# Image keys and values of two cross-attention layers: one level of seven products, or two nested levels with streamed weight operands

## The chip, the cores and the metric

The kernel runs on one core of a Trainium2 chip. The metric is the time of one execution on the device in microseconds (us). The kernel before was run three times, and the profile is one further execution of it, recorded by the hardware profiler. The engines are called PE (matrix products; PEld is its weight load), DVE (vector engine), ACT (scalar engine), POOL (GpSimd) and SP (which only issues DMAs here). L637 is line 637 of the kernel.

## The reference

Two cross-attention layers follow each other on `x` (8 batches, 100 queries, 640 channels). Both attend to the same context of 722 tokens of 1024 channels: 77 text tokens and 645 image tokens. There are 20 heads of 32 channels. Everything is fp32. Per layer, cut to what matters:

```
q = heads(x @ Wq)
k, v       = heads(text @ Wk), heads(text @ Wv)
k_ip, v_ip = heads(ip @ Wk_ip), heads(ip @ Wv_ip)     # 645 x 1024 times 1024 x 640, per batch
out = softmax(q k^T / sqrt(32)) v + softmax(q k_ip^T / sqrt(32) [+ sem / 2]) v_ip [* mask]
x   = out @ Wo + bias + x
```

The bracketed parts are in the second layer alone: `sem` is a score of the image tokens that comes from the text (softmax of q against the text keys over all channels, times the text, times the image tokens), and `mask` scales each query's image part. The image keys and values `k_ip`, `v_ip` don't depend on `x`. They are 2 layers x 8 batches x 2 products, the largest part of the arithmetic.

## The kernel before

**Seven products.** A product of two matrices, each cut into 2 x 2 quarters, can be had from seven products of quarters instead of eight, if sums of quarters are formed first and the results are summed afterwards. `seven` (L191 to L235) does this for one product. Its seven steps are named after the product they make, in the order 1, 6, 2, 7, 5, 4, 3, and they use five PSUM banks' names a, b, a, c, d, e, d: products 2 and 3 go on in the bank of 1 and 5. After each product the result leaves PSUM: by an ACT copy (L202, L211) or a DVE add with the partial result (L207, L217, L222, L228, L233). The sums of weight quarters (`weight_sums`, `w4_sums`, DVE) are made once per layer and stay in SBUF, the sums of token quarters (`block_sums`, `third_sum`, `fourth_sum`; L241, L242, L587, L599, DVE) once per block.

**Production.** The image tokens of a pair of batches (`PAIRS`) are the two halves of the rows. A pair has five blocks of tokens: four of 128 and a fifth of 133. `pair_tasks` lists its work. For v the tokens are the weight operand (128 x 128) and the weights move, 320 columns, or 397 where a text part lies beside them in layer 0 (L637). For k the weights are the weight operand and two blocks of tokens move, 256 columns, or 133 for the fifth block (L667). The fifth chunk of 128 output channels of k is made for both layers at once. Results go by POOL's DMA queue to DRAM (`v_d` at L652, `k_d` at L691 and L694). The last pair of layer 1 has its own order (`two_chunks`, `fifth_chunk`, L786 to L841). Pair 0 is made ahead of the attention; the others in it.

**Attention.** `ORDER` lists 80 iterations (u, c): u is one of 16 layer-and-batch units, c one of five chunks of four heads. An iteration loads k and v, makes the scores (L994), the softmax over text and image (DVE L1003 to L1057, ACT L1017 to L1049), the transposes (L1099, emptied by DVE L1106 or ACT L1104) and the product with v (L1122). The steps that have no product of PE in them are kept in a list `later`, and are emitted one at a time, so that they lie between products. The out projection (L904), the next layer's q (L923) and the `sem` steps are placed in fixed slots of iterations.

**Order.** The order of PE, DVE and ACT is the order of the program (`manual_schedule`). POOL's and SP's order is left to the scheduler. `production` gives each pair a stretch of ten iterations, shifted by `AHEAD` = 1.2; `spread` places its tasks there by estimated times, so that each iteration gets the same work. `next_task` emits one element of `later` before each product; `apart` lets one product come before a transposition or another small piece.

**PSUM.** Of the eight banks, two belong to products (`ps_pj`), two to transposes and other pieces of the attention (`ps_pt`), and four to scores. Before the attention the products have six (`ps_first`).

Of the kernel before, what the change touches and what calls it, by code (L numbers as in the profile page):

```python
# [36 lines left out]
BLOCKS = [(j * P, (j + 1) * P if j < NB - 1 else NI) for j in range(NB)]  # L37
NX = NI - (NB - 1) * P
# [8 lines left out]
def two_layer_xattn(  # L47
# [21 lines left out]
    wpool = ctx.enter_context(tc.tile_pool(name="w", bufs=1))  # L69
    cpool = ctx.enter_context(tc.tile_pool(name="ctx", bufs=2))  # L70
    spool = ctx.enter_context(tc.tile_pool(name="sums", bufs=1))
    opool = ctx.enter_context(tc.tile_pool(name="made", bufs=2))
    dram = ctx.enter_context(tc.tile_pool(name="scratch", bufs=1, space=bass.MemoryType.DRAM))

# [11 lines left out]

    ident = const.tile([P, P], F32, tag="ident", name="ident")
# [6 lines left out]
    W = {}  # L94

    def load_quarters(kind, src, n):

        rows = src.rearrange("(k p) n -> p k n", p=P)
        for i in range(2):
            for j in range(2):  # L100
                load_quarter(kind, rows, n, i, j)


    WITH_TEXT = ("wv00", "wv01", "wv10", "wvt4")
    wide = {}

    def weight_tile(tag, n, name=None):
        w = HC + NT if tag in WITH_TEXT else HC if tag[:2] == "wv" else n
        wide[tag] = wpool.tile([P, HK, w], F32, tag=tag, name=name or tag)
        return wide[tag][:, :, :n]  # L110

    def load_quarter(kind, rows, n, i, j):
        t = weight_tile(f"w{kind}{i}{j}", n)
        nc.sync.dma_start(t, rows[:, HK * i : HK * (i + 1), n * j : n * (j + 1)])
        W[kind, f"b{i + 1}{j + 1}"] = t

    def load_text(us):

        for i, (tag, h) in zip((0, 0, 1, 1), (("wv00", 0), ("wv10", 1), ("wv01", 0), ("wvt4", 1))):
            b = us[i] % B  # L120
            nc.sync.dma_start(
                wide[tag][:, :, HC:],
                text_t[HK * h : HK * (h + 1)].rearrange("k p n -> p k n")[:, :, b * NT : (b + 1) * NT],
            )

    def text_sum():
        t = wide["wvt4"][:, :, HC:]
        nc.gpsimd.tensor_tensor(t, t, wide["wv01"][:, :, HC:], ALU.subtract)

    def weight_sums(kind, n):  # L130

        b11, b12, b21, b22 = (W[kind, f"b{x}"] for x in ("11", "12", "21", "22"))
        t2, t3, t4 = (weight_tile(f"w{kind}t{x}", n) for x in (2, 3, 4))
        W[kind, "t1"], W[kind, "t2"], W[kind, "t3"], W[kind, "t4"] = b12, t2, t3, t4
        return [
            lambda: nc.vector.tensor_tensor(t3, b22, b12, ALU.subtract),
            lambda: nc.vector.tensor_tensor(t2, t3, b11, ALU.add),
            lambda: nc.vector.tensor_tensor(b12, b12, b11, ALU.subtract),
            lambda: nc.vector.tensor_tensor(t4, b21, t2, ALU.subtract),
        ]  # L140
# [4 lines left out]
    def load_wk(src):  # L145
        load_quarters("k", src, 2 * P)
        load_wk4(src)

    def load_wk4(src):
        W["k", 4] = wpool.tile([P, NCC, P], F32, tag="wk4", name="wk4")  # L150
# [3 lines left out]
    NPLACE = 3  # L154
    x_all = cpool.tile([P, NPLACE, 2, NCC, NX], F32, tag="x", name="x", bufs=1)
    placed = [0]

    s_all = spool.tile([P, 3, HK, 2, NX], F32, tag="s", name="s")

    def place_of(us, i):  # L160

        return (NB * PAIRS.index(us) + i) % NPLACE

    def quarters(at, n):
        return [x_all[:, at, i, HK * h : HK * (h + 1), :n] for i in range(2) for h in range(2)]

    def load_x(us, i):

        j = i % NB
        n0, n1 = BLOCKS[j]  # L170
        at = placed[0] % NPLACE
        placed[0] += 1
        for h, u in enumerate(us):
            nc.sync.dma_start(
                x_all[:, at, h, :, : n1 - n0], ip_t[u % B].rearrange("k p n -> p k n")[:, :, n0:n1]
            )
        assert at == place_of(us, i)
        return at

    ps_pj = ctx.enter_context(tc.tile_pool(name="ps_pj", bufs=2, space=PSUM))
    pj = []

    def product_ps(name):
        return pj[0].tile([P, 512], F32, tag="pj", name=name)

    def seven(name, product, area, beside=None):
# [6 lines left out]
        def flat(which):  # L195
            a = ps[which][:, :n]
            return a if len(c11.shape) == 2 else a.rearrange("p (r n) -> p r n", r=c11.shape[1])

        def first():
            ps["a"] = product_ps(f"{name}_a")  # L200
            product(ps["a"], 1, False)
            nc.scalar.copy(c11, flat("a"))  # L202

        def sixth():
            ps["b"] = product_ps(f"{name}_b")
            product(ps["b"], 6, False)
            nc.vector.tensor_tensor(c12, flat("b"), c11, ALU.add)  # L207

        def second():
            product(ps["a"], 2, True)  # L210
            nc.scalar.copy(c11, flat("a"))  # L211
            beside(2, ps["a"])

        def seventh():
            ps["c"] = product_ps(f"{name}_c")
            product(ps["c"], 7, False)
            nc.vector.tensor_tensor(c21, flat("c"), c12, ALU.add)  # L217

        def fifth():
            ps["d"] = product_ps(f"{name}_d")  # L220
            product(ps["d"], 5, False)
            nc.vector.tensor_tensor(c22, flat("d"), c21, ALU.add)  # L222
            beside(5, ps["d"])

        def fourth():
            ps["e"] = product_ps(f"{name}_e")
            product(ps["e"], 4, False)
            nc.vector.tensor_tensor(c21, flat("e"), c21, ALU.add)  # L228
            beside(4, ps["e"])

        def third():
            product(ps["d"], 3, True)
            nc.vector.tensor_tensor(c12, flat("d"), c12, ALU.add)  # L233

        return [first, sixth, second, seventh, fifth, fourth, third]  # L235

    TEXT_AT = {1: "wv00", 2: "wv10", 5: "wv01", 4: "wvt4"}
    WHICH = {1: "b11", 2: "b21", 3: "b22", 4: "t4", 5: "t1", 6: "t2", 7: "t3"}

    def token_sums(a11, a12, a21, a22, s1, s2, s3, s4):  # L240
        nc.vector.tensor_tensor(s1, a21, a22, ALU.add)  # L241
        nc.vector.tensor_tensor(s2, s1, a11, ALU.subtract)  # L242
        if s3 is not None:
            nc.vector.tensor_tensor(s3, a11, a21, ALU.subtract)
            nc.vector.tensor_tensor(s4, a12, s2, ALU.subtract)
        return {1: a11, 2: a12, 3: s4, 4: a22, 5: s1, 6: s2, 7: s3}

    def block_sums(us, j, pos):

        n = BLOCKS[j][1] - BLOCKS[j][0]  # L250
        a11, a12, a21, a22 = quarters(place_of(us, j), n)
        sums = [s_all[:, i, :, pos, :n] for i in range(3)]
        token_sums(a11, a12, a21, a22, sums[0], sums[1], None, sums[2])
# [4 lines left out]
    with ExitStack() as es:  # L258
        fp = es.enter_context(tc.tile_pool(name="first", bufs=1))
        pj.append(es.enter_context(tc.tile_pool(name="ps_first", bufs=6, space=PSUM)))  # L260
# [4 lines left out]
        for k in range(NC_):  # L265
            t = fp.tile([P, C], F32, tag="wr", name=f"wq0_{k}", bufs=NCC)
# [32 lines left out]
        for g in range(B // 2):  # L299
            t = fp.tile([P, 2, NC_, S], F32, tag="q", name=f"q0_{g}", bufs=2)  # L300
# [29 lines left out]
        def text_k(l):  # L330
            t = fp.tile([P, 2, 512], F32, tag="ev", name=f"kt4_{l}", bufs=2)
# [9 lines left out]
            for r in range(2):  # L341
                t = opool.tile([P, 2, 2, C // 2], F32, tag="made", name=f"kt_{l}_{r}")

                def product(ps, which, go_on, r=r):
                    for k in range(HK):
# [6 lines left out]
                for f in seven(  # L352
                    f"pskt_{l}_{r}", product, tuple(t[:, h, m, :TH] for h in range(2) for m in range(2))
# [7 lines left out]
        def text_v(l):  # L361

            t = fp.tile([P, 2, 512], F32, tag="ev", name=f"vtr_{l}", bufs=2)
# [17 lines left out]
        def text_v_blocks(l):  # L381
            for r in range(2):
                t = opool.tile([P, 2, 2, HC], F32, tag="made", name=f"vt_{l}_{r}")

                def product(ps, which, go_on, r=r):
                    for k in range(HK):
# [5 lines left out]
                for f in seven(f"psvt_{l}_{r}", product, tuple(t[:, h, m] for h in range(2) for m in range(2))):  # L392
# [6 lines left out]
        wl = {}  # L399

        def load_left(l):
            for k in range(NCC):
                wl[l, k] = fp.tile([P, C], F32, tag="wr", name=f"wl_{l}_{k}", bufs=NCC)
                nc.sync.dma_start(wl[l, k], wvi[l][k * P : (k + 1) * P, :])

        def left_v(l):

            ps = product_ps(f"psvl_{l}")
            for k in range(NCC):
                for m in range(2):  # L410
                    nc.tensor.matmul(
                        ps[64 * m : 64 * m + B * NL, :HC], lhsT=left_sb[:, k, :],
                        rhs=wl[l, k][:, m * HC : (m + 1) * HC],
# [27 lines left out]

        def all_of(parts):
# [3 lines left out]
        with tc.manual_schedule(engines=PINNED):  # L446
            text_sums()
            all_of(weight_sums("k", 2 * P))
            text_k(0)
            load_wk(wkt[1])  # L450
            v = weight_sums("v", HC)
            all_of(v[:2])
            text_v(0)
            all_of(v[2:])
            load_left(0)
            text_v_blocks(0)
            load_wv(wvt[1])
            all_of(weight_sums("k", 2 * P))
            text_k(1)
            load_quarters("k", wki[0], 2 * P)  # L460
            left_v(0)
            load_left(1)
            left_text()
            v = weight_sums("v", HC)
# [3 lines left out]
            for j in range(3):  # L468
# [960 lines left out]
```

## Time and profile before

| what | before |
|---|---|
| median of three runs | 2043.24 us (2042.67 to 2043.44) |
| span of the profiled execution | 2041.3 us |
| PE busy | 2024.2 us, 99%, clock 1.0 |
| DVE busy | 1129.4 us, 55% |
| ACT busy | 783.1 us, 38% |
| POOL busy | 274.2 us, 13% |
| DMA | 252.20 MB, mean 124 GB/s |
| PE, start to 205 us (q, text) | 202.98 busy |
| PE, 205 to 405 us (pair 0) | 198.41 |
| PE, 405 to 1341 us (iterations 0 to 39, layer 0) | 934.91 |
| PE, 1341 to 1909 us (iterations 40 to 69) | 565.64 |
| PE, 1909 us to the end | 122.21 |

The profiled execution's own time is its span, 2041.3 us; the median of the runs lies 1.9 us above it. A line of a timeline gives the start in us, the time for which the group was busy, the engine, the line of the kernel, the operation, the tiles (output <- inputs), the shape and how often; in brackets the idle time of the engine before it and what ended it. Several equal instructions in a row are merged into one line. Matmuls overlap: what one costs is the distance between starts, not its own duration. A line of the waits reads: engine, tile and line that waited, what ended the wait, total us, number, longest.

### The profile page before, as it was taken

The numbers are of one execution on the slowest core, as the hardware profiler recorded it, in microseconds if no ns is written. First come the engines' busy times: TensorE is split into PE (matmuls) and PEld (weight loads), VectorE is DVE, ScalarE is ACT, GpSimd is POOL, SyncE is SP. The second block draws the span as 40 slices with busy tenths as digits, with TensorE's granted clock in tenths as the row PEclk, the third lists the DMA queues.
The fourth block names the chain that finished last, engine by engine and source line by source line (L and its number), as shares of the span: only waits on it lengthen the run. The fifth ranks groups of instructions, "written<-read, shape, count | busy, mean of one in ns | idle before, by whom it ended". The sixth has DMA issues, their size and how long they took to land.

```text
span 2041.3 us, 38689 instructions
## 1 busy us (share of the span) xinstructions
PE 2024.2 (99%) x15162; PEld 1568.8 (77%) x15162; DVE 1129.4 (55%) x3048; ACT 783.1 (38%) x2245; POOL 274.2 (13%) x433
## 2 busy tenths in 40 slices
PE   9999999999999999999999999999999999999998
PEld 9676768776876867778678777777777778889877
DVE  2223322245555465554657665655665667778787
ACT  1001000033433343333434444444544455566676
POOL 0001212111111101111111001001010101111110
PEclk9999999999999999999999999999999999999999
DMA  9544323323432533325256354236342536545461
GB/s 341 154 131 147 108 75 93 99 66 93 117 99 71 157 102 108 89 83 156 90 131 172 92 164 121 82 100 183 99 118 81 148 95 174 147 138 152 124 189 55
DMA packets 296628, 252.20 MB, mean 124 GB/s; under 512 B 46654, under 2 KB 265586, under 8 KB 296446
## 3 DMA queue, kind: packets, MB, share of 16 engines
q1 hardware_dynamic: 274398, 181.19, 32.8%
q0 software_dynamic: 21776, 68.44, 9.3%
q8 instruction: 119, 1.95, 0.4%
q14 instruction: 63, 0.52, 0.1%
q10 hardware_dynamic: 272, 0.10, 0.0%
HBM read 180.74 MB, written 68.93 MB: 122 GB/s over the span
## 4 chain that ended last, share of the span: by engine, by line
PE 95%; DVE 4%; ACT 1%; issue 0%; DMA 0%; SPq 0%; DVEq 0%
PE psv_a L637 9%; PE psv_d L637 8%; PE pspt L1099 8%; PE psk_a L667 8%; PE psk_d L667 7%; PE sc L994 6%; PE psv_e L637 4%; PE pv L1122 4%; PE psk_b L667 4%; PE psk_c L667 4%; PE psv_b L637 4%; PE psv_c L637 4%; PE psk_e L667 4%; PE pso L904 3%; PE psq L923 2%; PE psq L305 2%
## 5 line engine op out<-in xcount | busy, mean ns | idle before, releaser
L1017 ACT ACTIVATE p<-sc,st 100x512 f32<-100x512 f32 (+1 forms) x320 | 165.8, 530 | 201.8 <-DVE st L1003 120.0
L1049 ACT ACTIVATE p<-p,st 100x512 f32<-100x512 f32 x318 | 206.7, 713 | 46.2 <-DVE st L1043 45.9
L1099 PEld LDWEIGHTS pspt<-ident,p 100*128 100x128 f32 (+1 forms) x1920 | 187.1, 137 | 42.7 <-issue 5.3
L1106 DVE COPY pt<-pspt 128x400 f32<-128x400 f32 (+1 forms) x319 | 175.2, 568 | 77.8 <-PE pspt L1099 69.4
L1099 PE MATMUL pspt<-ident,p 100*128 100x100 f32 (+1 forms) x1920 | 209.6, 250 | 6.5 <-DVE pt L1106 2.1
L1017 ACT ACTIVATE p<-p,st 100x512 f32<-100x512 f32 (+1 forms) x320 | 176.6, 554 | 76.8 <-DVE st L1009 76.8
L637 PE MATMUL psv_a<-wv,x 128*128 128x397 f32 (+1 forms) x560 | 185.9, 474 | 0.6 <-DVE ko L228 0.3
L1104 ACT COPY pt<-pspt 128x400 f32<-128x400 f32 x161 | 79.1, 491 | 249.3 <-PE pspt L1099 248.9
L637 PE MATMUL psv_d<-wv,s 128*128 128x320 f32 (+1 forms) x560 | 174.4, 454 | 0.0
L691 POOL DMA_DIRECT2D k_d<-ko x140 | 100.0, 718 | 453.2 <-DVE ko L228 399.8
L637 PEld LDWEIGHTS psv_a<-wv,x 128*128 128x128 f32 x560 | 102.8, 189 | 68.4 <-issue 13.6
L1009 DVE CUSTOM_DVE_ANT_0 p<-sc,sem 100x512 f32<-100x512 f32 (+1 forms) x320 | 138.7, 490 | 21.9 <-PE sc L994 21.0
L637 PEld LDWEIGHTS psv_d<-wv,s 128*128 128x128 f32 x560 | 103.5, 190 | 52.6 <-issue 3.3
L1003 DVE TENSOR_REDUCE st<-sc 100x2 f32<-100x1024 f32 (+1 forms) x160 | 125.2, 824 | 28.8 <-PE sc L994 28.7
L994 PE MATMUL sc<-k,q 32*100 32x210 f32 (+1 forms) x1280 | 138.5, 502 | 0.0
L667 PE MATMUL psk_d<-s,wk 128*128 128x256 f32 (+1 forms) x672 | 136.7, 348 | 0.1
L667 PE MATMUL psk_a<-x,wk 128*128 128x256 f32 (+1 forms) x672 | 135.2, 346 | 0.0
L667 PEld LDWEIGHTS psk_d<-s,wk 128*128 128x128 f32 x672 | 108.5, 189 | 20.7 <-issue 6.7
L667 PEld LDWEIGHTS psk_a<-x,wk 128*128 128x128 f32 x672 | 109.5, 189 | 17.7 <-issue 4.5
L652 POOL DMA_DIRECT2D v_d<-vo x70 | 38.8, 554 | 624.6 <-DVE gst L627 318.7
L637 PE MATMUL psv_e<-wvt,x 128*128 128x397 f32 (+1 forms) x280 | 92.9, 474 | 0.0
L1122 PEld LDWEIGHTS pv<-pt,v 128*32 128x32 f32 x3200 | 67.5, 110 | 26.2 <-issue 17.2
(218 smaller groups left out, 3301.2 us busy)
## 6 DMA issues: line engine op xcount, KB each, us to landing
x<-ip_t SPq DMA_DIRECT2D x80, 512.0 KB
k<-k_d SPq DMA_DIRECT2D x80, 322.5 KB
v<-v_d SPq DMA_DIRECT2D x80, 320.0 KB
v_d<-vo POOLq DMA_DIRECT2D x70, 320.0 KB, 2.4
k_d<-ko POOLq DMA_DIRECT2D x112, 128.0 KB, 4.4
o<-wo SPq DMA_DIRECT2D x35, 320.0 KB
x<-ip_t SPq DMA_DIRECT2D x20, 532.0 KB
q<-wq SPq DMA_DIRECT2D x20, 320.0 KB
```

What stands on the lines that cost most here:

```text
L637: nc.tensor.matmul(ps[:, :m], lhsT=tokens(k)[:, :P], rhs=w[:, k, :], start=(k == 0 and not go_on), stop=(k == HK - 1), skip_group_check=True,)
L667: nc.tensor.matmul(ps[:, i * m : (i + 1) * m], lhsT=w[:, k, :], rhs=tokens(k), start=(i == 0 and k == 0 and not go_on), stop=(k == HK - 1) ...
L691: nc.gpsimd.dma_start(dst[:, :, r], src)
L994: nc.tensor.matmul(scs[i // 2][:S, i % 2, : k1 - k0], lhsT=qs_[u][rows, c, :], rhs=ks[u, c][rows, k0:k1], start=True, stop=True)
L1003: nc.vector.tensor_reduce(st[:, part, 2 * h : 2 * h + 2], scs[h][:S, :, :n], AX.X, ALU.max, negate=True)
L1009: nc.vector.tensor_tensor_reduce(out=p[:, i, k0 : k0 + n], in0=scs[h][:S, i % 2, :n], in1=sems[u][:, k0 : k0 + n], scale=-1.0, scalar=3.0e ...
L1017: nc.scalar.activation(dst, dst if l else scs[h][:S, i % 2, :n], AF.Exp, bias=st[:, part, i : i + 1], scale=-1.0 if l else 1.0, accum_out= ...
L1049: nc.scalar.activation(p[:, i, :KA], p[:, i, :KA], AF.Copy, scale=mul[:, 0, i : i + 1])
L1099: nc.tensor.transpose(ps[:rows, i * S : (i + 1) * S], pr[u, c][:, i, j * P : j * P + rows], ident[:S, :S])
L1104: nc.scalar.copy(dst, src)
L1106: nc.vector.tensor_copy(dst, src)
L1122: nc.tensor.matmul(ps[32 * i : 32 * i + 32, :S], lhsT=lhs, rhs=pt[:rows, j, i * S : (i + 1) * S], start=(j == 0), stop=(j == 5),)
```

## The change

Production is made by two nested levels. An outer seven products (`OUTER` lists their order) cut a unit's tokens and weights into quarters, and each of them is made by an inner seven products of quarters of quarters, 49 for what were 64. Also:

- The fifth blocks of all eight batches of a layer become one unit ("b"); a pair's four blocks of 128 are another ("p"). `UNITS` is b0, p0 to p3, b1, p4 to p7. Units b0 and p0 are made ahead of the attention, with the two sets of four banks; the last one, p7, by one level (`last_tasks`), the fifth output chunk too (`fifth_steps`, 512 columns).
- An inner product of v is two times two Matmults of 160 columns (237 with text beside), one of k two of 256 (266 in a b unit).
- Sums of tokens for the outer level are made by DVE (`outer_piece`), those for the inner level by DVE in units 0 and 1 and by POOL in the others (`inner_sum`). The seven outer results are combined by POOL (`combined`).
- The weight operands, sums of both levels, are formed at the start, by POOL but for the outer sums of the first layer's k (`operand_sums`, `last_operands`, `fifth_sums`), and written to DRAM (`op_d`, `o5_d`, `ol_d`; text in `tx_d`). Each product's operand is then loaded from there through SP, into one of six buffers, five products ahead (`take`, `LOOK`). Layer 1's are formed between units 0 and 1.
- Products and the attention's pieces share four banks (`ps_b`). `apart` admits products up to an estimated 1.7 us, and an element of `later` is emitted after 1.3 us of products.
- Units 2 to 6 are spread over iterations -0.6 to 39.4, units 7 and 8 to 59.4, p7 to 74.4 and its fifth chunk to 78.4.

The diff, cut to its core:

```diff
+HV = HC // 2
+VT = HV + NT
+NW = 6
+OUTER = (1, 6, 2, 7, 5, 4, 3)
...
-    ps_pj = ctx.enter_context(tc.tile_pool(name="ps_pj", bufs=2, space=PSUM))
+    ps_b = ctx.enter_context(tc.tile_pool(name="ps_b", bufs=4, space=PSUM))
...
+    UNITS = [("b", 0)] + [("p", g) for g in range(4)] + [("b", 1)] + [("p", g) for g in range(4, 8)]
+    FIRST_BODY = 2
...
+    def inner_sum(n, i, which, engine):
+        a11, a12, a21, a22 = (quarter(n, i, t, q) for t in range(2) for q in range(2))
...
+        if which == 5:
+            engine.tensor_tensor(t, a21, a22, ALU.add)
...
+    def take(at):
+        while streamed[0] <= min(at + LOOK, len(stream) - 1):
+            t = prod.tile([P, 512], F32, tag="w", name=f"w_{streamed[0]}", bufs=NW)
+            made_w[streamed[0]] = stream[streamed[0]](t)
+            streamed[0] += 1
+        return made_w.pop(at)
...
+        def combined(what, i, x):
...
+                nc.gpsimd.tensor_tensor(
+                    to.rearrange("p a b n -> p (a b n)"), of.rearrange("p a b n -> p (a b n)"),
+                    other.rearrange("p a b n -> p (a b n)"), ALU.add,
+                )
...
+            def product(ps, j, go_on, part):
+                wt, (_, m), of = take(at[j][0]), at[j], inner_operand(n, i, j)
+                for o in range(2):
+                    for kc in range(2):
+                        nc.tensor.matmul(
+                            ps[:, o * pitch : o * pitch + m], lhsT=of[:, kc, o * w : o * w + P], rhs=wt[:, kc, :],
+                            start=(o == 0 and kc == 0 and not go_on), stop=(kc == 1), skip_group_check=True,
+                        )
...
+            def begun():
+                c = state["c"] = prod.tile([P, 2, 2, HC], F32, tag="cv", name=f"cv_{n}_{i}", bufs=4)
...
+                for kc in range(2):
+                    nc.tensor.matmul(
+                        ps[:, : 2 * w], lhsT=wt[:, kc, :], rhs=of[:, kc, :],
+                        start=(kc == 0 and not go_on), stop=(kc == 1), skip_group_check=True,
+                    )
...
+        for g2, i in enumerate(OUTER):
...
+            for s, task in enumerate(v_steps(i)):
...
+            for s, task in enumerate(k_steps(i)):
...
+            if not l:
+                tasks += fifth_steps(i)
...
+        def operand_sums(kind, l, inner_on, outer_on):
...
+                inner_on.tensor_tensor(t1, b[0, 1], b[0, 0], ALU.subtract)
+                inner_on.tensor_tensor(t3, b[1, 1], b[0, 1], ALU.subtract)
+                inner_on.tensor_tensor(t2, t3, b[0, 0], ALU.add)
+                inner_on.tensor_tensor(t4, b[1, 0], t2, ALU.subtract)
+                d = op_d[kind, l, i]
+                nc.gpsimd.dma_start(d[:, :4], t.rearrange("p s k n -> p s (k n)"))
...
+            for x, (_, f) in enumerate(made):
+                f()
...
+            left_v(1)
+            operand_sums("v", 1, nc.gpsimd, nc.gpsimd)
+            load_operands("k", 1)
+            operand_sums("k", 1, nc.gpsimd, nc.gpsimd)
+            last_operands()
+            for _, f in early:
+                f()
...
+        placed = spread(-0.6, n // 2 + 4.4, body)
+        placed += spread(n // 2 + 4.4, n - 10.6, later_)
+        chunks, fifth = last_tasks()
+        placed += spread(n - 10.6, n + 4.4, chunks)
+        placed += spread(n + 4.4, n + 8.4, fifth)
...
-            if todo[done[0]][0] and later:
-                emit(1)
+            if todo[done[0]][0]:
+                if later and since[0] >= 1.3:
+                    emit(1)
+                    since[0] = 0.0
+                since[0] += todo[done[0]][0]
```

## The prediction

> **What bounds the kernel now.** I read the page from the top: busy times, slices, chain; then what PE waited for, the engines in four stretches of the attention, and the timeline at places that price what the change adds.
>
> ```profile
> span 2041.3 us, 38689 instructions
> ...
> PE 2024.2 (99%) x15162; PEld 1568.8 (77%) x15162; DVE 1129.4 (55%) x3048; ACT 783.1 (38%) x2245; POOL 274.2 (13%) x433
> ...
> PEclk9999999999999999999999999999999999999999
> ...
> GB/s 341 154 131 147 108 75 93 99 66 93 117 99 71 157 102 108 89 83 156 90 131 172 92 164 121 82 100 183 99 118 81 148 95 174 147 138 152 124 189 55
> ```
>
> PE is busy for 99% at a granted clock of 1.0 and idle for 17 us in all. Next, what PE waited for, longest first (total us, times, longest), then four stretches (iterations 5 to 24, 45 to 49, 65 to 69, 75 to 79 of the 80).
>
> ```profile
> PE pspt L1099 <- DVE pt L1106: 2.1, 8, 0.6
> PE pspt L1099 <- DVE res L909: 2.0, 9, 0.6
> ```
>
> ```profile
> core 0: us, PE busy (x) PEld busy (x) DVE busy (x) ACT busy (x) POOL busy (x), PEclk, DMA share, GB/s
> 517.60:1007.50 489.90, 489.75 (x3512) 371.15 (x3508) 263.74 (x629) 187.14 (x547) 71.30 (x116) 1.00 0.37 108
> 1452.70:1552.20 99.50, 99.50 (x812) 76.81 (x809) 64.42 (x209) 49.48 (x138) 10.90 (x16) 1.00 0.37 106
> 1832.60:1908.50 75.90, 75.90 (x883) 67.90 (x879) 63.31 (x208) 48.35 (x137) 11.56 (x16) 1.00 0.52 143
> 1975.00:2031.00 56.00, 53.57 (x653) 44.04 (x650) 48.41 (x178) 43.02 (x124) 6.32 (x11) 1.00 0.27 76
> ```
>
> So time goes down with PE work only as long as nothing else becomes late. PE stays full with DVE at 83% (63.31 of 75.90) and has lost 4% with DVE at 86% (48.41 of 56).
>
> **PE work removed.** Each fp32 Matmult is two passes; a pass costs the distance between starts. From the timeline:
>
> ```profile
> 242.16 2.83 PE L637 MATMUL psv_a<-wv,x 128*128 128x397 f32 x8
> ...
> 244.83 2.31 PE L637 MATMUL psv_b<-wvt,s 128*128 128x320 f32 x8
> ...
> 205.47 1.89 PE L667 MATMUL psk_b<-s,wkt 128*128 128x256 f32 x8
> ...
> 207.20 1.89 PE L667 MATMUL psk_a<-x,wk 128*128 128x256 f32 x8
> ```
>
> Eight passes of 397 columns take 244.83 - 242.16 = 2.67 us, 333 ns each; 256 columns 1.73 us, 216 each. The same reading gives 269 for 320, 169 for 200, 113 for 133, 112 for 128. That is a line of 0.83 ns a column, so 160 columns cost 136 ns, 237 cost 200, 266 cost 224, and 512, extended from 397, 429. The nearest rows bound 160 at 113 and 169, but the line through both leaves 3 ns, 9 us in all.
>
> Before, counted from the program order (Matmults x two passes): v 320 of 397 and 660 of 320 columns, 568 us; k 1008 of 256 and 504 of 133, 549; last pair 280 of 133, 224 + 80 of 128 and 56 of 133, 144: 1261 us. After: v 1508 of 160 and 256 of 237, 512; k 196 of 266 and 686 of 256, 384; fifth output chunk 56 of 266 and 112 of 512, 121; text beside 64 of 77 at the 112 of 128 columns, 14; last pair 56 of 512 and 288 of 128, 112: 1143 us. PE loses **118 us**; text, queries, attention and outputs keep theirs. Floor: 2041.3 - 118 = 1923 us of span.
>
> **POOL and DVE, which get the work.** POOL issues 452 tensor adds instead of 6 (outer combinations, inner sums of units 2 to 8, all operand sums) and 370 DMAs. Its rows:
>
> ```profile
> 205.51 0.86 POOL L128 TENSOR_TENSOR wvt<-wvt,wv 128x308 f32<-128x308 f32 x1
> ...
> 1394.64 0.69 DVE L242 TENSOR_TENSOR s<-s,x 128x512 f32<-128x512 f32 x1
> 1394.69 2.50 POOL L948 TENSOR_TENSOR res<-res,bias_sb 128x500 f32<-128x500 f32 x2 [10.23 <-DMA res<-x_d]
> ```
>
> The two of 500 elements took 1.517 us, overlapping DVE's L242, and 1.017 alone, 2.03 ns an element. By that POOL's adds are 606 us and its DMA issues (554 ns for the 70 at L652, 718 for L691's) some 257, so 860 us of POOL, 433 of adds in the attention. The page GPSIMD Engine Reference of the Trainium skill (3.1) has 4497 ns for 2048 fp32 elements, 2.2 an element, which would make it 655 us.
>
> DVE: evictions become smaller and more numerous. A PSUM add of 320 columns costs 491 ns and one of 256 costs 424, so only 67 ns follow 64 columns. With the resident weight sums gone I count about +140 us: 1129 to 1270, still 65%.
>
> What I weigh most is that the two engines hold each other up. L1031 is a DVE add of two SBUF inputs, 4 elements wide: minimum and median 150 ns over its 80, yet
>
> ```profile
> 578.95 0.84 POOL L128 TENSOR_TENSOR wvt<-wvt,wv 128x308 f32<-128x308 f32 x1 [0.53 <-DMA wvt<-text_t]
> ...
> 579.46 0.35 DVE L1031 TENSOR_TENSOR st<-st 100x4 f32<-100x4 f32 x1
> ...
> 827.21 0.85 POOL L128 TENSOR_TENSOR wvt<-wvt,wv 128x308 f32<-128x308 f32 x1 [0.94 <-issue]
> ...
> 827.30 0.77 DVE L1031 TENSOR_TENSOR st<-st 100x4 f32<-100x4 f32 x1
> ```
>
> both slow ones run under a POOL add and end with it, within 20 ns. DVE adds with one PSUM input (L228) show no such thing. Section 8 of the same skill page names that case, contention with VectorE instructions of two SBUF inputs, and its section 4.1 puts elementwise adds on VectorE; both speak against this change.
>
> The price: seven such small adds per iteration (L1031 to L1057) and 16 outer sums per unit, seven units in 60 iterations: 8.9 an iteration. POOL adds fill 433 of some 1200 us, 36%, and one in progress has 0.87 us left on average (half of 0.65 to 2.6 us, the long ones met more often): 0.31 us each, **2.75 us of DVE per iteration**, from 0 (rows unlike these) to 5 (two in a row).
>
> **Where waits arise.**
>
> *Start: +28 (15 to 60).* Units 0 and 1 are made before the attention, and the operand sums of layer 1 stand between them in POOL's order: 55 adds (50 us by the price above) and 51 DMA issues (34), 85 us, and 12 more by holding. PE's list gives it about 10 us of other work and four chunk rounds of unit 1 (7 x 1.08 + 7 x 0.87 + 3.43 = 17.1 us each) before it needs a fifth v buffer, and there are four, freed by POOL's first combinations, which stand behind those sums: 79 us of cover for 85 + 12 + 10 for the freeing combination and its store.
>
> *Units 0 and 1: +12 (0 to 30).* The product that reuses a bank follows one product of 0.87 to 1.08 us later; before, the shortest distance was 1.73. Copy (426 ns) and add (491) fit with no queue ahead. All 56 such edges here are under 1.3 us; 0.2 us each. The stream reads 86 MB in 273 us, 315 GB/s, where the first slice moved 341.
>
> *Layer 0, iterations 0 to 39: +30 (5 to 60).* DVE reaches about 17.5 of 22 us, 80%, below the 83% that left PE full. But some 50 edges have under 1.3 us, and DVE's and ACT's fixed order puts one softmax step (L1009 490 ns, L1003 824) plus a hold ahead of the release: 0.6 us each.
>
> *Layer 1, units 7 and 8, 20 iterations: +30 (10 to 50).* Production is 49 x 1.08 + 49 x 0.87 = 96 us a unit, PE 16.4 us an iteration, down from 20. DVE: attention 9.9, evictions and sums 3.6, holds 2.75: 16.3. That is full. Without the holds it is 82%, which PE survived at 1832; at 86% the row at 1975 lost 4%, so at 99% I take 9% of 328 us.
>
> *Deadlines: +10 (0 to 20).* Units 6, 7 and 8 end at iterations 39.4, 49.4 and 59.4, and their k is first loaded at 39, 49 and 59: store and load (2.4 us landing for v, 4.4 for k) are exposed, 3 to 5 us each.
>
> *Stream later: +8 (0 to 90).* SP issues 1526 DMAs instead of 577, at about 0.4 us. Weights run five products ahead, 5 us; a small load lands 2.4 us after issue, but behind a 1 MB load or an issue that waits for its buffer it is late. Rows of before show neither, hence the wide end.
>
> *End: +6 (0 to 15).* One block is loaded again for the last fifth chunk while DVE is at 86%.
>
> Sum: 1923 + 28 + 12 + 30 + 30 + 10 + 8 + 6 = 2047 us of span; the median of the runs lies 1.9 above the span (2043.24 to 2041.3), so 2049, which I call **2050**: the PE work goes, and waits that weren't there take its place. What hides POOL's adds and the weight stream at no cost is PE's backlog; where it is under a product the whole delay shows.
>
> **Rivals.**
>
> *Faster: holds land in slack.* If DVE recovers within a bank's cover (four shared banks stand open where each kind had two), layer 0's 30 and layer 1's 30 shrink to 10 and the stream to 0: 1923 + 28 + 12 + 10 + 10 + 6 + 2 = 1991, and 1960 if the operand sums are covered too. For it: PE full at 83% DVE, and only two of 80 adds were ever held. Against: POOL added only 4 times there, so two is half of its chances. It decides if DVE stays below 85% in units 7 and 8.
>
> *Slower: the stream starves PE.* SP is in order; a weight load behind one that waits for its buffer stops all later ones. 2100 needs 58 us more than my sum, 1.5 us at 40 of the chunk rounds. For it: three times the issues, twice the bytes (252 to about 415 MB). Against: DMA share of 0.37 to 0.52 in the attention.
>
> *Slower: POOL is late.* Chunk buffers (four of each kind) wait for combinations. In units 2 to 8 POOL has about 60% to do; held by DVE as at 1394 (1.517 for 1.017) its adds grow by half, to 78%. At 100% PE would follow POOL, some 2120.
>
> **How the numbers follow.** Forecast's case 0.40 (2025 to 2085), holds in slack 0.36 (1955 to 2025), starved stream 0.14 (2080 to 2150), POOL late 0.10 (2080 to 2180). 0.2%, 4 us, is what a measurement can tell: faster is 0.36 plus 0.08 from the forecast's lower end, the same 0.07, slower the rest, 0.49. The range drops 0.1 at each end: 1965 to 2125.
>
> **What would show it.** PE busy about 1906 us and 160-column passes 136 ns apart confirm the removal. Holds: two-SBUF adds on DVE with medians over 250 ns and DVE over 95% in units 7 and 8. Start: a PE gap of 15 to 60 us in unit 1 behind POOL. Stream: PE waits on w by DMA below 15 us; more means the starved rival. Wrong would be PE over 97% busy, or a PE pass that isn't linear below 200 columns.

## The result and the profile after

The changed kernel takes 2226.69 us (median of 4 runs, 2224.6 to 2234.64), the kernel before 2043.34 in the runs beside it: a ratio of 1.0904, 95% interval 1.0885 to 1.0922. The forecast was 2050 with a range up to 2125. The profiled execution has a span of 2224.1 us, 182.8 more than before.

First the page of the changed kernel, the same lines as before.

```profile
span 2224.1 us, 42375 instructions
...
PE 1983.0 (89%) x15342; PEld 1595.4 (72%) x15342; DVE 1409.3 (63%) x3324; ACT 813.2 (37%) x2322; POOL 975.0 (44%) x828
...
PEclk9877999988999999999999999999999999999999
...
GB/s 349 166 198 231 96 178 190 191 266 269 263 173 177 184 180 159 212 195 208 167 178 214 204 197 189 218 187 206 183 200 196 188 189 193 204 163 127 138 149 56
```

PE is idle for 241 us, and from 56 to 222 us and 445 to 556 us (slices 2 to 4, 9 and 10) its granted clock is 0.7 to 0.8. The windows are the text stage, pair 0 (units 0 and 1), iterations 0 to 39, 40 to 59, and the rest (columns as in the prediction). First the kernel before, all but the rest:

```profile
0.00:205.00 205.00, 202.98 (x1046) 149.51 (x1047) 54.33 (x72) 20.80 (x49) 22.47 (x44) 1.00 0.62 194
205.00:405.40 200.40, 198.81 (x851) 147.56 (x850) 53.27 (x106) 11.76 (x33) 38.25 (x61) 1.00 0.31 94
405.40:1341.10 935.70, 934.61 (x6755) 708.95 (x6754) 528.15 (x1240) 371.11 (x1087) 126.03 (x202) 1.00 0.38 110
1341.10:1750.60 409.50, 409.16 (x3289) 321.73 (x3286) 262.80 (x845) 196.87 (x552) 48.80 (x71) 1.00 0.45 127
```

and the changed kernel:

```profile
0.00:266.80 266.80, 205.43 (x1008) 151.21 (x1009) 52.40 (x65) 19.92 (x47) 137.19 (x183) 0.88 0.64 211
266.80:647.30 380.50, 306.19 (x1569) 256.31 (x1567) 206.02 (x283) 26.89 (x68) 233.99 (x221) 0.92 0.71 223
647.30:1584.90 937.60, 873.77 (x6896) 709.74 (x6895) 645.93 (x1378) 387.47 (x1130) 429.28 (x300) 0.98 0.63 190
1584.90:1957.80 372.90, 345.82 (x3126) 284.93 (x3122) 295.73 (x868) 198.29 (x564) 154.86 (x100) 0.99 0.64 192
1957.80:2224.00 266.20, 251.81 (x2763) 193.21 (x2759) 209.23 (x731) 180.64 (x514) 19.64 (x26) 1.00 0.43 126
```

A busy PE still holds waits. So I add up, over all passes, the smaller of the distance to the next start and the pass's own cost by the prediction's line, and call the rest of a stage its excess: time in which PE waited, or ran a pass at a lower clock.

| stage | before: length, own, excess | after: length, own, excess | excess more |
|---|---|---|---|
| text | 205.0, 200.0, 5.0 | 266.8, 194.3, 72.5 | 67.5 |
| pair 0; units 0 and 1 | 200.4, 197.5, 2.9 | 380.5, 279.5, 101.0 | 98.1 |
| attention to the end | 1635.9, 1569.5, 66.4 | 1576.8, 1378.6, 198.2 | 131.8 |

Own work falls by 1967.0 - 1852.4 = 115 us, the excess grows by 297, and 297 - 115 = 182: that is the difference of the spans. The longest waits of PE (total us, times, longest):

```profile
PE psk_d L485 <- DVE ck L169: 60.4, 32, 9.8
PE psvt_a L822 <- ACT vt L166: 36.2, 1, 36.2
PE psk_d L485 <- DMA w<-op_dk: 19.6, 4, 12.1
PE pskt_a L781 <- ACT kt L166: 16.9, 1, 16.9
```

They name the places. `psk_d` is product 3, which goes on in the bank of product 5 after product 4 alone, and waits for DVE to have read it. `psvt` and `pskt` are the text stage's products. The timeline there:

```profile
91.92 2.32 PE L822 MATMUL psvt_b<-wvt,s_text 128*128 128x320 f32 x8
...
130.01 0.42 ACT L166 COPY vt<-psvt_a 128x320 f32<-128x320 f32 x1 [39.37 <-DMA op_dv<-iv]
130.47 0.49 DVE L169 TENSOR_TENSOR vt<-psvt_b,vt 128x320 f32<-128x320 f32 x1 [39.95 <-ACT vt L166]
...
130.49 4.64 PE L822 MATMUL psvt_a<-wv,text 128*128 128x320 f32 x8 [36.25 <-ACT vt L166]
```

The text's v result (`vt`) and the operand sums of layer 0 (`iv`) take turns in the same two buffers (tag "I"). The copy waits until the sixth of POOL's seven groups of sums has been stored; PE stands for 36 us, and its next eight passes take twice as long (4.64 against 2.32).

In units 0 and 1 PE waits 40.6 us for weight loads (`w` by DMA, the 19.6 above among them) and 33.6 us for DVE. The largest of both, and the longest wait for a load:

```profile
PE psk_d L485 <- DVE ck L169: 30.2, 10, 9.8
PE psv_e L439 <- DMA w<-op_dv: 6.9, 2, 3.6
PE psk_b L485 <- DMA w<-op_dk: 5.3, 1, 5.3
```

```profile
517.25 0.99 SPq L896 DMA_DIRECT2D olv<-wvi  x2
518.35 1.39 SPq L326 DMA_DIRECT2D w<-op_dk  x3
523.02 2.05 PE L485 MATMUL psk_d<-i,w 128*128 128x256 f32 x4 [12.06 <-DMA w<-op_dk]
```

The load of layer 1's weights (`olv`) waited 12.1 us on SP for a buffer that POOL's sums still held, and the stream's loads stood behind it. 25.5 of the 40.6 us are, like this one, waits for a load that follows one for layer 1's operand sums on SP, by at most eight places; what made the other 15 is not shown.

### The profile page after: what moved, and what is told of

Its sections match the earlier page's. It is cut to its first block, busy times and chain, and to the rows that moved or that the text cites. A ratio compares the mean times of both kernels' runs of the same rounds, so it can differ in the third digit from the quotient of the medians.

```text
span 2224.1 us, 42375 instructions
## 1 busy us (share of the span) xinstructions
PE 1983.0 (89%) x15342; PEld 1595.4 (72%) x15342; DVE 1409.3 (63%) x3324; ACT 813.2 (37%) x2322; POOL 975.0 (44%) x828
## 4 chain that ended last, share of the span: by engine, by line
PE 62%; DVE 15%; POOL 8%; DMA 7%; issue 5%; ACT 2%; SPq 0%; DVEq 0%; POOLq 0%; ACTq 0%
PE pspt L1353 6%; PE psv_d L439 5%; PE psf L514 5%; PE psv_a L439 5%; PE sc L1248 4%; PE psk_d L485 4%; PE pv L1376 4%; PE psk_a L485 3%; PE pso L1157 3%; PE psv_e L439 3%; PE psv_c L439 2%; DMA w<-op_dv 2%; PE psv_b L439 2%; DVE st L1257 2%; PE psq L740 2%
## 5 line engine op out<-in xcount | busy, mean ns | idle before, releaser
L398 POOL TENSOR_TENSOR cv<-cv,cv 128x1280 f32<-128x1280 f32 x63 | 186.0, 2952 | 427.2 <-DVE cv L169 296.9
L485 PE MATMUL psk_d<-i,w 128*128 128x256 f32 (+1 forms) x504 | 148.7, 421 | 81.8 <-DVE ck L169 60.4
L439 PE MATMUL psv_d<-w,i 128*128 128x160 f32 (+1 forms) x1008 | 173.9, 316 | 25.1 <-issue 16.7
L439 PEld LDWEIGHTS psv_d<-w,i 128*128 128x128 f32 x1008 | 151.0, 193 | 45.0 <-issue 34.4
L485 PEld LDWEIGHTS psk_d<-i,w 128*128 128x128 f32 x504 | 96.9, 204 | 120.0 <-DVE ck L169 76.3
L398 POOL TENSOR_TENSOR ck<-ck,ck 128x1024 f32<-128x1024 f32 (+1 forms) x63 | 156.8, 2489 | 46.6 <-DVE ck L169 37.5
L166 ACT COPY cv<-psv_a 128x320 f32<-128x320 f32 x126 | 53.4, 424 | 265.8 <-PE psv_a L439 219.9
L439 PE MATMUL psv_a<-w,a 128*128 128x160 f32 (+1 forms) x576 | 105.3, 325 | 3.7 <-ACT cv L166 3.7
L439 PEld LDWEIGHTS psv_a<-w,a 128*128 128x128 f32 x576 | 89.9, 190 | 18.1 <-issue 5.6
L1376 PE MATMUL pv<-pt,v 128*32 128x100 f32 x3200 | 87.7, 256 | 5.3 <-DVE pt L1360 3.7
```

What stands on the lines that cost most here:

```text
L398: nc.gpsimd.tensor_tensor(to.rearrange("p a b n -> p (a b n)"), of.rearrange("p a b n -> p (a b n)"), other.rearrange("p a b n -> p (a b n ...
L439: nc.tensor.matmul(ps[:, o * pitch : o * pitch + m], lhsT=of[:, kc, o * w : o * w + P], rhs=wt[:, kc, :], start=(o == 0 and kc == 0 and no ...
L485: nc.tensor.matmul(ps[:, : 2 * w], lhsT=wt[:, kc, :], rhs=of[:, kc, :], start=(kc == 0 and not go_on), stop=(kc == 1), skip_group_check=True,)
L1376: nc.tensor.matmul(ps[32 * i : 32 * i + 32, :S], lhsT=lhs, rhs=pt[:rows, j, i * S : (i + 1) * S], start=(j == 0), stop=(j == 5),)
```

## The experiments

The stage lengths, read from the first product of unit 0 and the first scores, tell where an edit acted. Times are medians where there was more than one run (before, after, e6, e12). Where an edit leaves a stage alone, its length says how much differs without a cause: in the attention 1574 to 1581 us, in the text stage 266 to 268, in units 0 and 1 380 to 386.

| run | what | time | text | units 0, 1 | attention |
|---|---|---|---|---|---|
| before | | 2043.3 | 205.0 | 200.4 | 1635.9 |
| after | | 2226.7 | 266.8 | 380.5 | 1576.8 |
| e1 | text results in own tiles | 2204.4 | 243.8 | 384.5 | 1574.3 |
| e2 | e1, eight loads by POOL | 2212.1 | 245.0 | 386.6 | 1578.4 |
| e3 | no outer combination | 2186.2 | 267.2 | 383.0 | 1534.2 |
| e4 | no POOL adds in the attention | 2153.6 | 266.5 | 384.4 | 1500.9 |
| e5 | no operand sums of layer 1 | 2187.0 | 266.6 | 337.5 | 1581.1 |
| e6 | operand sums on DVE | 2199.6 | 243.3 | 373.5 | 1577.1 |
| e7 | e4, a bank for product 3 | 2130.3 | 268.1 | 371.3 | 1489.1 |
| e8 | combination on DVE | 2213.5 | 266.9 | 386.1 | 1558.7 |
| e9 | no adds in operand sums | 2149.5 | 212.4 | 358.7 | 1576.6 |
| e10 | e9, no DVE sums in units 0, 1 | 2127.0 | 219.3 | 328.9 | 1577.0 |
| e11 | e7, a bank for product 2 too | 2087.3 | 241.2 | 363.3 | 1481.1 |
| e12 | four mends, nothing left out | 2137.2 | 225.4 | 361.9 | 1541.4 |
| e13 | e10 and e11 | 2024.1 | 200.6 | 340.8 | 1480.9 |

**The text stage.** e1 gives the text's results tiles of their own.

```diff
-t = fp.tile([P, 2, 2, HC], F32, tag="I", name=f"vt_{l}_{r}", bufs=2)
+t = [[prod.tile([P, HC], F32, tag=f"i{h + 1}", name=f"vt_{l}_{r}_{h}{m}", bufs=2) for m in range(2)] for h in range(2)]
```

> The text stage of layer 0 and 1 puts its keys and values into two buffers that POOL's operand sums use as well (tag I); here they get buffers of their own, nothing else changes. Theory (shared buffers): the gaps of 36.2, 6.5 and 16.9 us before 198 us of the changed kernel go, PE's text stage ends near 210 us of span instead of 267, and the span falls from 2224 by 45 to 60 us. Rival (the wait only moves): POOL is late with the operands of unit 0 anyway, PE then waits at the start of unit 0 for its weights, and the span falls by less than 20 us.

The stage became 23 us shorter, not 55: the shared buffers are one cause. The rest is still there (excess 49): ACT waits 27.7 us for a store of the new tiles (`vt_d`), and these stores are POOL's as well and stand behind the same sums. e9 left out the adds (POOL's, and DVE's four outer ones) and kept every load and store; as the inner sums need no tile then, the shared buffers are free too:

```diff
-inner_on.tensor_tensor(t1, b[0, 1], b[0, 0], ALU.subtract)
...
-inner_on.tensor_tensor(t4, b[1, 0], t2, ALU.subtract)
 d = op_d[kind, l, i]
-nc.gpsimd.dma_start(d[:, :4], t.rearrange("p s k n -> p s (k n)"))
+nc.gpsimd.dma_start(d[:, :4], o.rearrange("p k q n -> p (k q n)").rearrange("p (s m) -> p s m", s=4))
```

> Leaves out the adds of the operand preparation (112 inner and 16 outer ones, and the last pair's four), but keeps every load and store of it: the stores write raw weights. Values are wrong, products are as many and as long. Theory (the adds' time on POOL, with DVE's adds held meanwhile, makes the start long): the text stage ends near 225 us instead of 267, units 0 and 1 take 320 to 335 us instead of 380, the span falls by 80 to 110 us. Rival (queues and buffers: stores and loads in POOL's and SP's order, however short the adds): the span falls by less than 50 us.

The stage falls to 212 us. So 54 of its 67.5 us go when the adds and their use of the buffers go, of which e1 had shown 23 for the buffers alone; units 0 and 1 fell by 22 only, and the whole by 77, just under the theory's range.

**Units 0 and 1.** e5 leaves out layer 1's operand sums.

```diff
-operand_sums("v", 1, nc.gpsimd, nc.gpsimd)
-load_operands("k", 1)
-operand_sums("k", 1, nc.gpsimd, nc.gpsimd)
-last_operands()
```

> Leaves out the operand sums of layer 1 between units 0 and 1 and their loads (57 POOL adds, 51 DMA issues); layer 1's units read layer 0's operands and the last unit raw weights, so the products after unit 1 are as many and as long but of wrong values. Theory (POOL's operand sums hold DVE's inner sums, and stand ahead of the combinations): PE's waits and slow clock in units 0 and 1 (101 us in the changed kernel, 267 to 647 us) fall to 35 to 55, the span by 45 to 70. Rival (the stream's bandwidth and the short distances between products that share a bank): they fall by less than 25 us.

43 us of the 101 go and 40 of the whole, a little less than expected. Most of the 43 is not DVE's: PE's waits for weight loads fall from 40.6 to 17.4 us, those for DVE from 33.6 to 24.6. e9, which kept layer 1's loads and stores, had left 34.2 of waits for loads. Two other causes were tried. e2 moved the loads that wait for operand buffers from SP's queue to POOL's:

```diff
-                    nc.sync.dma_start(
+                    nc.gpsimd.dma_start(
                         b[i, j].rearrange("p k r n -> p k (r n)"),
```

> As e1, and the eight loads that wait for operand buffers between units 0 and 1 (k and the last pair's v of layer 1) are issued by POOL, so that no weight load of the stream stands behind them on SP. Theory (SP's queue holds the stream up): PE's waits for w by DMA in units 0 and 1 (39 us in the changed kernel, the longest 12.1) fall below 10, and the span falls by 25 to 40 us more than in e1. Rival (bandwidth, or POOL's lateness, sets units 0 and 1): less than 10 us more than in e1.

It failed: units 0 and 1 took as long, and the whole 8 us longer than e1. The waits for w fell from 46.9 (e1) to 33.2 us, not below 10, and those for DVE rose from 30.1 to 44.0. e10, on top of e9, took DVE's own sums and the text differences away:

```diff
+if n < FIRST_BODY:
+    INNER[n, i, which] = a11
+    return
```

> As e9, and the inner token sums of units 0 and 1 and the text differences on DVE are left out as well. Theory (DVE's own adds, 8 to 10 us of text differences at once and four sums per outer product, delay the evictions in units 0 and 1): a further 25 to 40 us, PE's wait for DVE's ck there goes from 28 to below 10. Rival (the stream: loads from DRAM are late at 255 to 315 GB/s): less than 12 us more than e9, with PE waiting for w by DMA for 20 us or more.

A further 30 us in that stage (22 of the whole, as the text stage came out 7 longer), and PE's wait for DVE's ck in it fell from 27.8 (e9) to 5.7. The timeline of the changed kernel shows one such place; the text differences, 7 us of DVE with a wait of 2.36 between, stand ahead of the evictions:

```profile
292.91 2.72 DVE L965 TENSOR_TENSOR text_d<-text 128x2464 f32<-128x2464 f32 x1
295.55 2.79 DVE L968 TENSOR_TENSOR text_d<-text 128x1232 f32<-128x1232 f32 x2
300.69 1.44 DVE L972 TENSOR_TENSOR text_d<-text_d 128x1232 f32<-128x1232 f32 x1 [2.36 <-DMA tx_d<-text_d]
302.05 0.43 DVE L169 TENSOR_TENSOR ck<-psk_c,ck 128x266 f32<-128x266 f32 x1
```

PE's product 3 then started at 304.12, 9.84 us late. e6 put all operand sums on DVE, in pieces between products, and layer 1's loads on POOL:

```diff
-            operand_sums("v", 1, nc.gpsimd, nc.gpsimd)
...
+                yield from operand_sums("v", 1, nc.vector, nc.vector)
+                load_operands("k", 1)
+                yield from operand_sums("k", 1, nc.vector, nc.vector)
+                yield from last_operands()
...
+                if x > 24 and x % 4 == 0:
+                    fill(1)
```

> All operand sums on DVE in pieces of two adds between the products of the text stage and of units 0 and 1, and layer 1's loads by POOL; nothing is left out. Theory (it is POOL, its in-order queue and its holding of DVE, that makes the start long): the text stage ends near 210 us instead of 267, units 0 and 1 take 300 to 330 us instead of 380, the span falls by 90 to 125 us. Rival (the work is too much for either engine there; it moves to DVE, whose evictions then come late): it falls by less than 50 us.

27 us less (ratio to before 1.0765, 1.0747 to 1.0783): the rival was right. In these two orders the work is in the way on either engine.

**The attention.** e3 and e4 leave out POOL's adds: e3 the combinations, by the edit below, and e4 the inner sums of tokens as well.

```diff
 def add(to, of, other):
+    if n >= FIRST_BODY:
+        return
     nc.gpsimd.tensor_tensor(
```

> Leaves out the outer combinations of units 2 to 8 on POOL (98 adds of 1024 to 1280 elements, about 265 us of POOL); PE, DVE, ACT and the DMAs keep their work. Theory (POOL's adds hold DVE's adds, and its lateness holds chunk buffers): PE's waits in the attention (165 us of 181 over its own time) fall by half or more, the span by 50 to 90 us. Rival (short distances between a bank's uses and the fixed order of DVE and ACT make the waits, whatever POOL does): the span falls by less than 25 us.

> As e3, and the inner token sums of units 2 to 8 on POOL are left out too (164 adds of 512 elements; the products read the tokens instead). No POOL add is left in the attention. Theory (POOL): the span falls by 90 to 130 us against the changed kernel and PE waits in the attention like before, 50 us. Rival (short distances, fixed order): it falls by less than 45 us and PE still waits for DVE's ck and ACT's cv at the products psk_d and psv_a. Between the two, the share that goes with POOL is read from it.

The attention shortened by 43 us without the combinations and by 76 without any POOL add; both spans fell less than the theory said, more than the rival. The windows of e4 (iterations 0 to 39, 40 to 59), to be set beside those of 937.60 and 372.90:

```profile
651.00:1540.00 889.00, 854.45 (x6897) 699.92 (x6901) 581.12 (x1379) 387.37 (x1130) 59.08 (x89) 1.00 0.67 200
1540.00:1886.00 346.00, 338.61 (x3122) 282.07 (x3126) 263.39 (x868) 198.72 (x565) 15.79 (x22) 1.00 0.69 206
```

How POOL reaches DVE is seen in one softmax add (before, changed, e4; minimum/median/maximum ns of its 80):

```profile
L1040 DVE TENSOR_TENSOR st<-st x80: 150/155/160, 423.5 to 2029.5; 100x8 f32<-100x8 f32 x80
```

```profile
L1294 DVE TENSOR_TENSOR st<-st x80: 151/156/2376, 670.9 to 2212.5; 100x8 f32<-100x8 f32 x80
```

```profile
L1299 DVE TENSOR_TENSOR st<-st x80: 150/155/930, 669.0 to 2140.3; 100x8 f32<-100x8 f32 x80
```

Of the 560 operations of DVE with two SBUF inputs in the softmax (seven per iteration; the prediction calls them adds), 67 were over 60 ns above their median, together 78 us; before 2, in e4 1. So holds are real. e8 asks what they are worth against the work itself, by moving the combinations to DVE:

```diff
-nc.gpsimd.tensor_tensor(
+(nc.vector if n >= FIRST_BODY else nc.gpsimd).tensor_tensor(
```

> The changed kernel with the outer combinations of units 2 to 8 on DVE instead of POOL (98 adds of 1024 to 1280 elements, about 133 us of DVE work by the DVE rows of 1220 and 1485 ns). Theory (a POOL add costs by what it holds and delays): the span lies within 30 us of 2224, since DVE's work replaces holds of about 80 us and late buffers. Rival (DVE's own load sets the attention): slower by 50 us or more.

13 us less in one run, where the changed kernel's four spread over 10; the attention itself is 18 shorter. DVE does them at no more cost than the holds and the lateness of POOL had. e7 and e11 then gave products 3 and 2 banks of their own, on top of e4. Product 3's costs one more DVE add per seven, product 2's turns an ACT copy into a DVE add.

```diff
-step(5, "d", False, lambda: added(c22, "d", c21), lambda: beside(5, ps["d"])),
+step(5, "d", False, lambda: added(c22, "d", c21), lambda: added(c12, "d", c12), lambda: beside(5, ps["d"])),
-step(3, "d", True, lambda: added(c12, "d", c12)),
+step(3, "f", False, lambda: added(c12, "f", c12)),
```

and, in e11,

```diff
-step(2, "a", True, lambda: copied("a"), lambda: beside(2, ps["a"])),
+step(2, "g", False, lambda: added(c11, "g", c11), lambda: beside(2, ps["g"])),
```

> As e4 (no POOL adds in the attention), and product 3 of every seven gets a bank of its own instead of going on in that of product 5, for one more DVE add of 256 to 512 columns per seven. Theory (what is left of the waits, 105 us against 44 before, is the short distance between the two uses of that bank): the attention's waits fall from 105 to below 80, the span by 20 to 40 us below e4's 2152. Rival (DVE's and ACT's fixed order makes evictions late whatever the bank): no change within 10 us, or slower by the 112 adds.

> As e7, and product 2 has a bank of its own too, added by DVE instead of copied by ACT (its text part is then incomplete, values are wrong). Theory (the second short distance, a bank used again after one product): the attention's waits fall from 93 us (e7) to below 75, psv_a and psk_a stop waiting for ACT. Rival (what is left is DVE's and ACT's order): within 8 us of e7, or slower by the DVE adds.

In the attention 12 and 8 us, less than expected of the first and at the rival's edge of the second; of both together the larger part fell in the text stage and units 0 and 1 (11 and 35 us). In units 0 and 1 PE's wait for DVE all but goes (34.5 us in e4, 4.7 in e7), yet that for weight loads grows from 39.9 to 60.4: two thirds of the gain are lost to the stream there. The places can be seen in the changed kernel's timeline:

```profile
674.99 1.03 PE L485 MATMUL psk_b<-i,w 128*128 128x256 f32 x4
676.77 1.13 PE L485 MATMUL psk_a<-s,w 128*128 128x256 f32 x4 [0.76 <-ACT ck L166]
```

One k product of 0.87 us lies between the two uses of bank a; the ACT copy came 0.76 us late.

**Together.** e12 keeps the whole computation, with e1, e8 and the two banks (product 2 only where no text lies beside).

> The changed kernel, all of its computation kept, with what helped in the other runs: text results in tiles of their own (e1: 22 us), products 2 and 3 in banks of their own where no text lies beside (e7 and e11: 23 and 43 us, there without POOL adds), outer combinations of units 2 to 8 on DVE (e8: 13 us). Theory (the causes add up): 2226 less 22, 13 and 40 to 66, so 2125 to 2150 us, still slower than before. Rival (the extra DVE adds of the banks and the combinations meet): 2170 or more.

2137 us, ratio to before 1.0463 (1.0446 to 1.0481): the mends add up and are still 94 us short. In its units 0 and 1 PE waits 53.6 us for weight loads and 2 for DVE, so the stream is most of what is left there. e13 leaves everything out at once.

> All of the ablations at once: no operand adds, no inner token sums and text differences in units 0 and 1 (e10), no POOL adds in the attention and two banks more (e11). All products, stores, loads and evictions are there, values are wrong. Theory (the stage sums are complete: own PE time 1852 us, waits of e10's start 17 to 24 and 40 to 50, and of e11's attention 88): 2000 to 2015 us, below before. Rival (something else holds the change up, such as the stream): 2040 or more.

```profile
span 2022.3 us, 42034 instructions
...
PE 1927.6 (95%) x15342; PEld 1572.0 (78%) x15342; DVE 1302.1 (64%) x3532; ACT 763.7 (38%) x2184; POOL 323.6 (16%) x410
```

Between the two, near the theory: 19 us below before (one run). One wait is more than the difference to the 2000 to 2015 expected. PE's waits, then SP's timeline:

```profile
PE psv_f L447 <- DMA w<-op_dv: 33.2, 3, 32.8
```

```profile
225.82 22.19 SPq L896 DMA_DIRECT2D olv<-wvi  x4
248.10 0.49 SPq L313 DMA_DIRECT2D w<-op_dv  x1
```

Four loads that wait for operand buffers stand on SP ahead of the weight load, and PE waits 32.8 us behind them. This is the queue that e2 had suspected. In the changed kernel the longest such wait is 12.1 us; that lateness of POOL and DVE hid the rest there is likely, as the waits for loads grow in e7, e11 and e12, but not shown.

## Why the prediction was wrong

*Right.* The direction, and the PE work removed: 115 us against 118. Its sign, PE busy about 1906 us, failed (1983), since a busy PE holds waits and slow passes. The price of 160 columns holds: of the changed kernel, eight passes from 663.84 to 664.93 us,

```profile
663.84 1.25 PE L439 MATMUL psv_a<-w,s 128*128 128x160 f32 x8
664.93 1.25 PE L439 MATMUL psv_b<-w,i 128*128 128x160 f32 x8
```

136 ns each; 512 columns take 429. DVE with holds was put at 1270 + 165 = 1435 us and measured 1409; that the sum came near is luck in part. The 165 us were for 60 iterations, 2.75 each. There the softmax has 77 us of holds (67 of 560, 1.16 us each, where 0.31 was put on every one) and DVE's sums of tokens 19, some 1.6 an iteration. Another 59 us lie on DVE's sums in units 0 and 1, where none had been put on DVE (an estimate: what these sums took beyond 690 ns at 512 elements and 717 at 532).

*The step that failed: "Start: +28" and "Units 0 and 1: +12".* Measured 67.5 + 98.1 = 166: of the 177 us by which the span passed its sum of 2047, 126 are here. Three mistakes. Layer 1's sums alone were priced; layer 0's, in the text stage, were left at nothing, with no look at which buffers the text's results share with them (54 of 67.5 us by e9). The cover of 79 us was counted as if PE ran at full rate beside 85 us of POOL: units 0 and 1 need DVE for their inner sums, which POOL's adds lengthen and which stand ahead of the evictions (33.6 us of waits; 30 us go with DVE's own sums, e10). And the stream was put at nothing in this stage, because its bandwidth would do: PE waits 40.6 us for weights there, 25.5 of them behind layer 1's loads on SP (23 go with these sums and loads, e5). The sign named, one gap of 15 to 60 us in unit 1, is not there; the waits are many, the longest 12.1 us.

*"Layer 0, iterations 0 to 39: +30 (5 to 60)".* Its excess grew from 24 to 118 us, by some 93, beyond the upper end. POOL's adds are 49 of it (937.6 to 889.0, e4), the banks 19 more (869.9 in e11). "DVE at 83% left PE full" was the wrong row: there a product of 1.8 us (1836.21 to 1838.05) and pieces of the attention lay between a bank's uses, here often one product of 0.87 to 1.09, and DVE at 69% (645.93 of 937.60) is late. The term was mis-sized: 0.6 us for each of some 50 short distances, where POOL's adds alone cost 49 us.

*"Layer 1, units 7 and 8: +30" with "Deadlines: +10".* 39 measured for both, DVE at 79% rather than full, so the number was met and the reason was not; e4 takes 27 of it away. *"End: +6"*: 0. *"Stream later: +8"*: PE's waits for w after 647 us are under 3 us in all.

*The rivals.* No case of the prediction reaches 2227 us. The starved stream names a cause that the runs show, weight loads behind one that waits for its buffer, and by the sign given for it (PE waits on w above 15 us) it is there; but all but some 2 us of it lies before the attention. It is 40.6 us of the 182.8 and more once DVE is relieved, so it isn't the whole. POOL late (2120, chance 0.10) named the right engine, but the price was put in units 2 to 8 and not at the start.

*Open.* With every POOL add gone and two more banks, the attention still has 36 us more excess than before (102.5 against 66.4). Short distances to other banks and the fixed order of DVE and ACT may be it; no run takes them apart. The weight loads' waits in units 0 and 1 (53.6 us in e12) were never taken away: e2 moved eight loads to POOL's queue, and another order on SP was not tried.

## What to carry to other kernels

A scheme that saves products pays in sums, evictions and shorter distances, and its saving should be weighed against all of them at the place where they land: here 115 us of PE against 297 of new waits and slow passes, more than half of them before the attention. Ask of each preparation which buffers, which queue and which engine's order it shares with the work it is meant to hide under; 85 us beside 79 us of cover was not free, because the cover itself needed DVE and the load queue. When products get shorter, the utilisation at which the evicting engine was harmless before is no longer a guide: look at the time between two uses of a bank.

## What the runs showed of the hardware

Operations with two SBUF inputs on the two engines lengthen each other. In the changed kernel POOL's add of 256 elements took 0.71 us alone, and beside DVE's adds of 1024 elements (1.23 us with no POOL add beside) both took longer:

```profile
165.06 0.71 POOL L860 TENSOR_TENSOR ik<-ok 128x256 f32<-128x256 f32 x1 [3.92 <-DMA op_dk<-ik]
...
168.10 1.23 DVE L872 TENSOR_TENSOR ok<-ok,ok 128x1024 f32<-128x1024 f32 x1 [8.02 <-POOL ik L863]
...
172.02 1.53 POOL L860 TENSOR_TENSOR ik<-ok 128x256 f32<-128x256 f32 x1 [0.96 <-DMA op_dk<-ik]
172.89 1.74 DVE L123 TENSOR_TENSOR wkt<-wk,wk 128x1024 f32<-128x1024 f32 x1
173.53 1.69 POOL L861 TENSOR_TENSOR ik<-ok 128x256 f32<-128x256 f32 x1
```

This is the contention that the Trainium skill names (GPSIMD Engine Reference, 8), with a price. All POOL adds together took 741 us, 606 were predicted. The shortest of each size lie near 0.17 us and 2.11 ns an element (0.712 us at 256, 1.254 at 512, 2.872 at 1280); the prediction's 2.03 ns, from a row of 500 elements, has no fixed part. By that line the adds would be some 700 us (an estimate), and the other 40 are probably holds. One of the seven softmax operations, of 532 elements (L1311), was never held (706 to 716 ns); why is open. The reciprocal between them, which has one input, was not held either (202 to 205 ns).

Waits cost twice where they are long. Around the gap of 36 us in the text stage (the windows, with the granted clock third from the end, then the passes after it):

```profile
94.00:130.00 36.00, 0.24 (x1) 0.00 (x0) 0.00 (x0) 0.00 (x0) 35.84 (x38) 0.57 0.52 175
130.00:140.00 10.00, 9.51 (x24) 6.35 (x25) 0.98 (x2) 0.85 (x2) 9.56 (x15) 0.68 0.86 279
...
134.91 3.10 PE L822 MATMUL psvt_c<-wvt,s_text 128*128 128x320 f32 x8
137.85 2.32 PE L822 MATMUL psvt_d<-wv,s_text 128*128 128x320 f32 x8
```

The first eleven passes of 320 columns after the gap, from 130.49 to 136.50, start some 533 ns apart instead of 269. Counted over the changed kernel, passes that start 1.9 to 2.1 times their own cost apart add 37 us (before 7). The Trainium skill (TensorE: Matmul & The Clock Gate, "What's actually happening") has the clock halve after at least one idle window of some 3.4 us and return after at least one busy one as long. The 6.0 us of slow passes here agree with that, as more than one such window and less than two.
